# Spreading the dense steps of four tiles among the gathered blocks of the other sixteen in a two-layer graph network

## The chip, the cores and the metric

The kernel runs on one core of one Trainium2 chip. The metric is the device time of one execution in microseconds (us). Several executions are timed and their median is taken; one more execution is recorded by the hardware profiler.

## What is computed

The input is a node matrix x of 2500 rows and 1024 columns, 80,000 edges (`src`, `dst`, `edge_weight`, sorted by `dst`), and two 1024 x 1024 weights. The destinations are drawn as the square of a uniform number, so that low rows receive many edges and high rows few. Two layers follow each other:

```python
h = relu(layernorm(x))
x = x + segment_sum((h @ W0)[src] * edge_weight[:, None], dst)      # layer 0
h = relu(layernorm(x)) @ W1.T + b
deg = 1 + count of edges with row = src
x = x + segment_sum(norm[:, None] * h[col], row)                    # layer 1, with self loops
# row, col = src, dst and the self loops; norm = deg[row] ** -0.5 * deg[col] ** -0.5
```

Everything is float32.

## The kernel before, in words

The 2500 rows are 20 tiles of 128 rows (the last has 68). The work runs in four parts.

The first part, up to about 477 us, normalises each tile of x, multiplies it by W0 (`products`, L277) and stores the result to `support` in DRAM. At the same time the edges are laid out in blocks of 128 edges, each block belonging to one destination tile. `TILE_BLOCKS` gives the number of blocks of each tile: 146, 62, 48 and 41 for tiles 0 to 3, then 36 down to 10 for tiles 4 to 19.

The second part aggregates layer 0. It visits the tiles in `ORDER`. Each has an accumulator `sums` of 128 x 1024 in PSUM (two banks, pool name `mm`, two such buffers). There are two ways to fill it:

- The tiles 4 to 19 (378 blocks in all) are **gathered**. For each block GpSimd issues an indirect DMA that brings 128 rows of `support` into a `msg` buffer of 512 KB (L558). VectorE makes a one-hot matrix `oh_r` (L562); ScalarE multiplies the rows by the edge weights and rounds to `hi` (L564); VectorE makes the rest `lo` (L566); TensorE multiplies the one-hot matrix with both, in halves of 512 columns: four matmuls (L570).
- The tiles 0 to 3 are **dense**. For them a matrix of 128 destination rows by 2500 source rows has been counted and weighted beforehand (`dense`). For each of 20 source tiles SyncE loads 512 KB of `support` into a `msg` buffer of the same eight, and TensorE does two float32 matmuls (L583). A dense step has no work for VectorE, ScalarE or GpSimd.

When a tile's sums are complete, `finish` adds them to x (`xt`, L539), stores x1, takes the moments and normalises (`hn`, L140), transposes (L530, through the PSUM buffers `pT`), multiplies by W1 (sixteen float32 matmuls, L277, into a buffer `mm`), adds the bias (L549) and stores `hid`. `finish` is a generator: its pieces are issued among the steps of the next tile.

Throughout the first two parts VectorE also counts edges per pair of rows (`count_group`, L432, L434, L444, with matmuls L436 and, for dense tiles, L448). `count` decides by a small clock model (`takes`) when the next group of blocks is counted. `fences` with `BEHIND` keep a step's first matmul behind the counts that were issued five steps earlier.

The third part (L645 to L649) reads `hid` back, scales it by `dis` and splits it in `hi` and `lo`. The fourth (L675) multiplies the stored counts with them, tile by tile, and writes the output.

The order of the work in the second part is thus written out in Python by the loops over `ORDER`; the framework's scheduler then settles each engine's instruction order, the buffers and the waits. SyncE issues all plain DMAs of this part in one queue: `msg` loads of dense steps, `xt` loads, the stores of x1 and `hid`, and the stores of counts (`cnat`). GpSimd issues the gathers.

Of the kernel before, what the change touches and what calls it, by code (L numbers as in the profile page):

```python
# [9 lines left out]
F32 = mybir.dt.float32  # L10
# [9 lines left out]
P = 128  # L20
# [12 lines left out]
DENSE = 4  # L33

LEAD = 4.0

BEHIND = 5

ORDER = (3, 4, 5, 6, 2, 7, 8, 9, 1, 10, 11, 12, 13, 0, 14, 15, 16, 17, 18, 19)

# [2 lines left out]
def direct(  # L43
# [26 lines left out]
    nc = tc.nc  # L70
    N, D = x.shape
    E = src.shape[0]
    NT = -(-N // P)
# [59 lines left out]
    def normed(xt, pool):  # L133
        mv = moments(xt, pool)
        rstd = pool.tile([P, 2], F32, name="rstd")
        nc.scalar.activation(rstd[:, 0:1], mv[:, 1:2], AF.Sqrt, bias=eps)
        nc.vector.reciprocal(rstd[:, 0:1], rstd[:, 0:1])
        nc.vector.scalar_tensor_tensor(rstd[:, 1:2], mv[:, 0:1], -1.0, rstd[:, 0:1], op0=ALU.mult, op1=ALU.mult)
        hn = pool.tile([P, D], F32, name="hn")
        nc.scalar.activation(hn, xt, AF.Relu, scale=rstd[:, 0:1], bias=rstd[:, 1:2])  # L140
        return hn
# [132 lines left out]
    def product(vT, ws, mm):  # L274
        for h in range(2):
            for k in range(KC):
                on_pe(nc.tensor.matmul(mm[:, h, :], vT[:, k, :], ws[k][:, h * H:(h + 1) * H],  # L277
                                       start=(k == 0), stop=(k == KC - 1)))
                if k % 2:
                    yield  # L280
# [192 lines left out]
    def left(queue):  # L473
        return sum(b - a for _, _, a, b in queue)
# [56 lines left out]
            nc.scalar.copy(into[:, k0:k0 + 4, :], pT)  # L531
            yield 0.7, 0.0, 0.6

    PIECES = 11

    def finish(t, sums):

        xt = load_rows(t, work)
        nc.vector.tensor_add(xt, sums.rearrange("p h d -> p (h d)"), xt)  # L539
        nc.sync.dma_start(x1_d[t], xt)  # L540
        hn = normed(xt, work)
        yield 0.0, 3.4, 1.5
        vT = work.tile([P, KC, P], F32, name="vT")
        yield from transposed(hn, vT)
        mm = psum.tile([P, 2, H], F32, name="mm")
        for _ in product(vT, w1_sb, mm):
            yield 1.75, 0.0, 0.0
        hid = work.tile([P, D], F32, name="hn")
        nc.vector.tensor_add(hid, mm.rearrange("p h d -> p (h d)"), bias)  # L549
        nc.sync.dma_start(hid_d[t], hid)  # L550
        takes(v=1.25)

    def gathered(t, sums):
        n = TILE_BLOCKS[t]
# [32 lines left out]
                    on_pe(i)  # L587
            yield 1.75, 0.0, 0.0

    waiting = iter(())  # L590
    todo, steps = left(to_count[1]), [NT * 4 if t < DENSE else TILE_BLOCKS[t] for t in ORDER]
    done = 0
    w1_sb = []
    for t in ORDER:
        sums = psum.tile([P, 2, H], F32, name="mm")
        pieces = 0.0
        for took in (multiplied if t < DENSE else gathered)(t, sums):
            k = len(w1_sb)
            if k < KC:
                w1_sb.append(wpool.tile([P, D], F32, name=f"w{k}"))  # L600
                nc.sync.dma_start(w1_sb[k], w1t[k * P:(k + 1) * P, :])
            pieces += 1.15 * PIECES / (NT if t < DENSE else TILE_BLOCKS[t])
            done += 4 if t < DENSE else 1
            while pieces >= 1:
                takes(*next(waiting, (0.0, 0.0, 0.0)))
                pieces -= 1
            count(*took, least=todo * (1 - 1.05 * done / sum(steps)))
        for took in waiting:
            takes(*took)
        if t == ORDER[0]:  # L610
            nc.sync.dma_start(bias, b1.rearrange("(o d) -> o d", o=1).to_broadcast([P, D]))
        waiting = finish(t, sums)
    for queue in to_count:
        while queue:
            count_next(queue)
    store_counts(late=False)
    for _ in waiting:
        pass


    nc.vector.tensor_reduce(deg, total, axis=mybir.AxisListType.X, op=ALU.add)
# [399 lines left out]
```

## Time and profile before

| what | us |
|---|---|
| median of 3 executions | 1795.9 (1795.83 to 1800.01) |
| the profiled execution | 1796.9 |
| its span in the trace | 1795.0 |
| TensorE busy | 1685.8 |
| VectorE busy | 1209.5 |
| ScalarE busy | 900.2 |
| GpSimd busy | 494.5 |
| first dense matmul starts | 482.4 |
| last W1 product ends | 1407.2 |

The ends of the tiles in the second part can be read from the starts of the add to x (L539): 529.7 for the dense tile 3, then 591.0, 647.6 and 696.4 for tiles 4 to 6, 753.3 for the dense tile 2, and so on up to 1386.2 for tile 19.

The profile names a line of the code, an engine, an operation and the tiles it writes and reads. A float32 matmul shows as two records. The busy time of TensorE comes from modelled ends of matmuls that overlap, so the distance between the starts of neighbouring matmuls tells more about its speed than the length of one. "Granted clock" is the share of TensorE's full clock in a window. A line "A <- B: t, n, m" in a list of waits says that A stood idle for t us in all, n times, at most m us, until B had finished.

### The profile page before, as it was taken

Reading aid. Unit: us, or ns where it says so; the run is one execution under the profiler, and the core shown is the slowest. Engines: PE = TensorE matmul, PEld = TensorE weight load, DVE = VectorE, ACT = ScalarE, POOL = GpSimd, SP = SyncE. Lnnn points to the kernel's source line nnn. Section 1 sums busy time; section 2 is a strip of 40 time slices with the busy share of each in tenths; the row PEclk is TensorE's granted clock in tenths of the full one; section 3 lists DMA queues with packets and bytes.
Section 4 is the critical chain, followed back from the end, with each engine's and each line's share of the span. In section 5 each row is a group of like instructions: output and inputs, shape, how many; then the busy total and the mean of one; then the engine's idle time right before and its main releaser. Section 6 shows DMA issues by size and latency. Waiting matters only on the chain.

```text
span 1795.0 us, 21337 instructions
## 1 busy us (share of the span) xinstructions
PE 1685.8 (94%) x6506; PEld 1047.4 (58%) x6506; DVE 1209.5 (67%) x3031; ACT 900.2 (50%) x1476; POOL 494.5 (28%) x457
## 2 busy tenths in 40 slices
PE   6999999999899999999999999989998999999998
PEld 2465655544345555456645555455554668888886
DVE  5887988898698997999988997188886330000000
ACT  3499999961136773276515665166564431111110
POOL 3000000000036771377416773266661000000000
PEclk9999999999899999999999999999999999999999
DMA  7513121132788999799979999788884764242420
GB/s 255 191 40 97 48 77 60 39 83 71 244 285 319 366 340 324 229 338 328 348 242 323 321 315 333 246 307 312 310 300 167 216 191 104 77 114 76 115 62 32
DMA packets 217330, 369.97 MB, mean 206 GB/s; under 512 B 115662, under 2 KB 135128, under 8 KB 217206
## 3 DMA queue, kind: packets, MB, share of 16 engines
q0 software_dynamic: 54832, 199.25, 31.9%
q1 hardware_dynamic: 162374, 169.25, 30.3%
q8 instruction: 54, 0.88, 0.2%
q14 instruction: 70, 0.57, 0.1%
HBM read 300.79 MB, written 54.56 MB: 198 GB/s over the span
## 4 chain that ended last, share of the span: by engine, by line
PE 53%; DVE 7%; DMA 1%; issue 1%; ACT 1%; DVEq 0%; ACTq 0%
PE mm L675 18%; PE mm L570 14%; PE mm L277 13%; PE mm L583 5%; DVE lo L566 3%; DMA rows<-hid_d 1%; PE pT L530 1%; DVE stats L128 1%; DVE xt L539 1%; PE cb L436 1%; DVE lo L649 1%; DVE oh_r L562 0%; ACT hi L647 0%; DVE counts L444 0%; DVE hn L549 0%
## 5 line engine op out<-in xcount | busy, mean ns | idle before, releaser
L558 POOL DMA_INDIRECT msg<-support,src_p x378 | 479.1, 1268 | 493.6 <-PE cb L436 129.0
L564 ACT ACTIVATE hi<-msg,wgt_p 128x1024 fp32r<-128x1024 f32 x378 | 424.2, 1147 | 315.8 <-PE mm L570 194.3
L566 DVE SCALAR_TENSOR_TENSOR lo<-msg,wgt_p,hi 128x1024 fp32r<-128x1024 f32 x378 | 477.0, 1279 | 78.6 <-ACT hi L564 77.0
L570 PE MATMUL mm<-lo,oh_r 128*128 128x512 f32 x756 | 285.1, 459 | 37.8 <-DVE lo L566 37.5
L277 PE MATMUL mm<-w,hT 128*128 128x512 f32 x640 | 317.4, 608 | 2.4 <-ACT hT L169 2.4
L277 PE MATMUL mm<-w,vT 128*128 128x512 f32 x640 | 307.6, 594 | 0.0
L570 PE MATMUL mm<-hi,oh_r 128*128 128x512 f32 x756 | 291.4, 468 | 15.5 <-DVE oh_r L562 9.9
L441 ACT ACTIVATE wl<-oh_low,wpart 128x128 bf16<-128x128 bf16 x891 | 261.9, 410 | 0.0
L675 PE MATMUL mm<-hi,bT 128*128 128x512 f32 (+1 forms) x800 | 249.2, 394 | 3.6 <-ACT bT L657 2.0
L675 PE MATMUL mm<-lo,bT 128*128 128x512 f32 (+1 forms) x800 | 249.4, 394 | 3.0 <-DVE lo L649 2.6
L663 DVE SCALAR_TENSOR_TENSOR rows<-mm,dis,rows 128x1024 f32<-128x1024 f32 x20 | 25.7, 1283 | 309.0 <-PE mm L675 308.9
L570 PEld LDWEIGHTS mm<-lo,oh_r 128*128 128x128 f32 x756 | 139.9, 197 | 127.8 <-DVE lo L566 83.1
L570 PEld LDWEIGHTS mm<-hi,oh_r 128*128 128x128 f32 x756 | 147.2, 199 | 99.4 <-ACT hi L564 41.3
L434 DVE TENSOR_SCALAR oh_key<-iota,key 128x200 bf16<-128x200 f16 (+12 forms) x675 | 193.1, 289 | 3.1 <-PE cb L448 2.8
L444 DVE TENSOR_TENSOR counts<-cb,counts 128x200 f32 (+13 forms) x296 | 138.5, 469 | 59.1 <-PE cb L436 52.8
L657 ACT CAST bT<-cT 128x2560 fp32r<-128x2560 f16 x20 | 46.6, 2335 | 262.2 <-PE mm L675 258.8
L675 PEld LDWEIGHTS mm<-lo,bT 128*128 128x128 f32 (+1 forms) x800 | 150.6, 190 | 39.5 <-DVE lo L649 8.1
L675 PEld LDWEIGHTS mm<-hi,bT 128*128 128x128 f32 (+1 forms) x800 | 151.4, 190 | 37.2 <-ACT bT L657 2.4
L277 PEld LDWEIGHTS mm<-w,vT 128*128 128x128 f32 x640 | 121.0, 190 | 86.6 <-issue 71.8
L432 DVE TENSOR_SCALAR oh_low<-iota,low 128x128 bf16<-128x128 f16 x675 | 164.6, 247 | 6.9 <-PE cb L436 5.5
L583 PE MATMUL mm<-msg,dense 128*128 128x512 f32 (+1 forms) x320 | 150.1, 599 | 5.6 <-DMA msg<-support 5.2
L277 PEld LDWEIGHTS mm<-w,hT 128*128 128x128 f32 x640 | 109.2, 195 | 64.6 <-issue 58.0
(141 smaller groups left out, 1135.2 us busy)
## 6 DMA issues: line engine op xcount, KB each, us to landing
msg<-support SPq DMA_DIRECT2D x76, 512.0 KB, 5.2
xt<-in_x SPq DMA_DIRECT2D x38, 512.0 KB, 7.1
cnat<-counts SPq DMA_DIRECT2D x20, 640.0 KB, 5.6
x_d<-xt SPq DMA_DIRECT2D x20, 512.0 KB, 7.4
hid_d<-hn SPq DMA_DIRECT2D x20, 512.0 KB, 6.2
rows<-hid_d SPq DMA_DIRECT2D x20, 512.0 KB, 4.5
rows<-x_d SPq DMA_DIRECT2D x20, 512.0 KB, 4.3
hT<-in_xT SPq DMA_DIRECT2D x19, 512.0 KB, 4.4
```

The lines of the kernel that those rows point to most:

```text
L277: on_pe(nc.tensor.matmul(mm[:, h, :], vT[:, k, :], ws[k][:, h * H:(h + 1) * H], start=(k == 0), stop=(k == KC - 1)))
L432: nc.vector.tensor_scalar(oh_low, iota16[:, :P], low[:, k:k + 1], None, op0=ALU.is_equal)
L434: nc.vector.tensor_scalar(oh_key[:, :NT * w], iota16[:, :NT * w], key[:, k:k + 1], None, op0=ALU.is_equal)
L441: nc.scalar.activation(wl[:, i, :], oh_low, AF.Copy, scale=wpart[:, i, k:k + 1])
L444: nc.vector.tensor_tensor(to, cb[:, :NT * w].rearrange("p (t w) -> p t w", w=w), to, op=ALU.add)
L558: nc.gpsimd.indirect_dma_start(out=msg, out_offset=None, in_=support, in_offset=bass.IndirectOffsetOnAxis(ap=src_p[:, k:k + 1], axis=0))
L564: nc.scalar.activation(hi, msg, AF.Copy, scale=wgt_p[:, k:k + 1])
L566: nc.vector.scalar_tensor_tensor(lo, msg, wgt_p[:, k:k + 1], hi.bitcast(F32), op0=ALU.mult, op1=ALU.subtract)
L570: i = nc.tensor.matmul(sums[:, h, :], oh, v[:, h * H:(h + 1) * H], start=(j == 0 and v is hi), stop=(j == n - 1 and v is lo))
L583: i = nc.tensor.matmul(sums[:, h, :], dense[t][:rows(k), k, :], msg[:rows(k), h * H:(h + 1) * H], start=(k == 0), stop=(k == NT - 1))
L657: nc.scalar.copy(bT, cT)
L675: nc.tensor.matmul(mm[:, h, :], bT[:rows(k), k, :], v[:rows(k), h * H:(h + 1) * H], start=(k == ORDER[0] and v is his[k]), stop=(k == ORDE ...
```

## The change

The loop over `ORDER` is replaced by a plan. `thick` are the dense tiles and `thin` the gathered ones, each in the order of `ORDER`. The plan is a list of booleans, true for a dense step: eight dense steps first (`OPENING`), then after the blocks of each thin tile a number of dense steps in proportion to its blocks, all used up 48 blocks before the last one (`TAIL`). Of a tile's dense steps all but two are spread between its blocks, and two follow its last block. Two generators deliver the steps of the two kinds, so that one dense and one gathered `sums` are open at the same time.

`finish` now runs its first piece (the load of x, the add and the store of x1) as soon as the last step of a tile is issued; the rest goes into a list `waiting`, from which pieces are taken at a rate that allows for the dense tiles finished meanwhile. The product with W1 goes by halves of 512 columns, each in one of the two `pT` banks, each with its own add of the bias, instead of one `mm` buffer of two banks and one add of 1024 columns.

The loads of W1, issued with the first steps before, are issued with the eight steps after the eight dense ones; the load of `bias` follows them.

```diff
+OPENING = 8
+TAIL = 48
...
-    PIECES = 11
+    PIECES = 12
 
     def finish(t, sums):
 
         xt = load_rows(t, work)
         nc.vector.tensor_add(xt, sums.rearrange("p h d -> p (h d)"), xt)
         nc.sync.dma_start(x1_d[t], xt)
+        yield 0.0, 1.25, 0.0
         hn = normed(xt, work)
-        yield 0.0, 3.4, 1.5
+        yield 0.0, 2.2, 1.5
         vT = work.tile([P, KC, P], F32, name="vT")
         yield from transposed(hn, vT)
-        mm = psum.tile([P, 2, H], F32, name="mm")
-        for _ in product(vT, w1_sb, mm):
-            yield 1.75, 0.0, 0.0
         hid = work.tile([P, D], F32, name="hn")
-        nc.vector.tensor_add(hid, mm.rearrange("p h d -> p (h d)"), bias)
+        for h in range(2):
+            mm = psum.tile([P, 4, P], F32, name="pT").rearrange("p a b -> p (a b)")
+            for k in range(KC):
+                on_pe(nc.tensor.matmul(mm, vT[:, k, :], w1_sb[k][:, h * H:(h + 1) * H],
+                                       start=(k == 0), stop=(k == KC - 1)))
+                if k % 2 and k < KC - 1:
+                    yield 1.75, 0.0, 0.0
+            nc.vector.tensor_add(hid[:, h * H:(h + 1) * H], mm, bias[:, h * H:(h + 1) * H])
+            if h == 0:
+                yield 1.75, 0.65, 0.0
         nc.sync.dma_start(hid_d[t], hid)
-        takes(v=1.25)
+        yield 1.75, 0.65, 0.0
...
-    waiting = iter(())
-    todo, steps = left(to_count[1]), [NT * 4 if t < DENSE else TILE_BLOCKS[t] for t in ORDER]
+    thick, thin = [t for t in ORDER if t < DENSE], [t for t in ORDER if t >= DENSE]
+    blocks = sum(TILE_BLOCKS[t] for t in thin)
+    plan = [True] * OPENING
+    rate = [0.0] * OPENING
     done = 0
+    for t in thin:
+        n = TILE_BLOCKS[t]
+        done += n
+        m = min(DENSE * NT, OPENING + -(-(DENSE * NT - OPENING) * done // (blocks - TAIL))) - sum(plan)
+        inner = max(m - 2, 0)
+        for j in range(n):
+            plan.append(False)
+            plan += [True] * ((j + 1) * inner // n - j * inner // n)
+        plan += [True] * (m - inner)
+        rate += [1.1 * PIECES * (1 + m / NT) / (n + m)] * (n + m)
+    assert sum(plan) == DENSE * NT
+
+    waiting = []
+    todo = left(to_count[1])
     w1_sb = []
-    for t in ORDER:
-        sums = psum.tile([P, 2, H], F32, name="mm")
-        pieces = 0.0
-        for took in (multiplied if t < DENSE else gathered)(t, sums):
-            k = len(w1_sb)
-            if k < KC:
+
+    def steps_of(tiles):
+        for t in tiles:
+            sums = psum.tile([P, 2, H], F32, name="mm")
+            n = NT if t < DENSE else TILE_BLOCKS[t]
+            for j, took in enumerate((multiplied if t < DENSE else gathered)(t, sums)):
+                if j == n - 1:
+                    rest = finish(t, sums)
+                    takes(*next(rest))
+                    waiting.append(rest)
+                yield took
+
+    kinds = {True: steps_of(thick), False: steps_of(thin)}
+    pieces = 0.0
+    for i, is_dense in enumerate(plan):
+        took = next(kinds[is_dense])
+        if i == OPENING:
+            for k in range(KC):
                 w1_sb.append(wpool.tile([P, D], F32, name=f"w{k}"))
-                nc.sync.dma_start(w1_sb[k], w1t[k * P:(k + 1) * P, :])
-            pieces += 1.15 * PIECES / (NT if t < DENSE else TILE_BLOCKS[t])
-            done += 4 if t < DENSE else 1
-            while pieces >= 1:
-                takes(*next(waiting, (0.0, 0.0, 0.0)))
-                pieces -= 1
-            count(*took, least=todo * (1 - 1.05 * done / sum(steps)))
-        for took in waiting:
-            takes(*took)
-        if t == ORDER[0]:
+        if i >= OPENING and (i - OPENING) < KC:
+            nc.sync.dma_start(w1_sb[i - OPENING], w1t[(i - OPENING) * P:(i - OPENING + 1) * P, :])
+        if i == OPENING + KC:
             nc.sync.dma_start(bias, b1.rearrange("(o d) -> o d", o=1).to_broadcast([P, D]))
-        waiting = finish(t, sums)
+        pieces = min(pieces + rate[i], 2.0) if waiting else 0.0
+        while pieces >= 1 and waiting:
+            piece = next(waiting[0], None)
+            if piece is None:
+                waiting.pop(0)
+                continue
+            takes(*piece)
+            pieces -= 1
+        count(*took, least=todo * (1 - 1.05 * (i + 1) / len(plan)))
...
-    for _ in waiting:
-        pass
+    for rest in waiting:
+        for _ in rest:
+            pass
```

## The prediction

> **What bounds the kernel now.** I first read the busy shares on the page, then a table of windows cut at the ends of tiles, then TensorE's waits, then the order of time around one tile's end.
>
> ```profile
> PE 1685.8 (94%) x6506; PEld 1047.4 (58%) x6506; DVE 1209.5 (67%) x3031; ACT 900.2 (50%) x1476; POOL 494.5 (28%) x457
> ```
>
> TensorE looks full, but the share hides that it alternates between two kinds of hunger. In the table by tiles (busy time of PE, PEld, DVE, ACT, POOL, then granted clock, DMA share, GB/s):
>
> ```profile
> 591.00:647.00 56.00, 51.56 (x182) 33.25 (x183) 55.33 (x88) 40.95 (x39) 43.18 (x36) 0.97 0.95 353
> ...
> 696.00:753.00 57.00, 56.80 (x170) 26.10 (x169) 45.40 (x145) 9.43 (x8) 8.43 (x9) 1.00 0.77 249
> ...
> 1114.00:1164.00 50.00, 50.00 (x125) 22.74 (x124) 7.87 (x14) 5.00 (x6) 8.66 (x10) 1.00 0.77 265
> ...
> 1204.00:1242.00 38.00, 34.42 (x120) 21.08 (x118) 32.85 (x47) 23.98 (x24) 25.82 (x21) 1.00 0.89 311
> ```
>
> Row 591 is gathered tile 5: VectorE is busy 55.3 of 56 us, TensorE waits, DMA moves 353 GB/s. Rows 696 and 1114 are dense tiles 2 and 0: TensorE is full, VectorE idles 11.6 and 42.1 us, DMA is at 0.77. The change mixes these two. What TensorE waits for from 482 to 1409 us:
>
> ```profile
> PE mm L570 <- DVE lo L566: 37.5, 56, 1.9
> PE mm L570 <- DVE oh_r L562: 9.9, 18, 0.7
> PE mm L583 <- DMA msg<-support: 5.2, 1, 5.2
> PE pT L530 <- ACT hn L140: 5.1, 1, 5.1
> PE mm L570 <- ACT hi L564: 4.3, 1, 4.3
> ```
>
> With three small rows this is 65.6 us. Where it falls is seen in TensorE's order of time at the end of tile 15:
>
> ```profile
> 1243.81 0.70 PE L570 MATMUL mm<-hi,oh_r 128*128 128x512 f32 x2 [0.69 <-DVE oh_r L562]
> 1246.10 0.73 PE L570 MATMUL mm<-lo,oh_r 128*128 128x512 f32 x2 [1.59 <-DVE lo L566]
> ...
> 1247.56 1.22 PE L570 MATMUL mm<-lo,oh_r 128*128 128x512 f32 x2 [0.26 <-DVE lo L566]
> 1248.58 1.05 PE L570 MATMUL mm<-hi,oh_r 128*128 128x512 f32 x2
> 1249.43 1.05 PE L570 MATMUL mm<-lo,oh_r 128*128 128x512 f32 x2
> ```
>
> VectorE adds the finished tile to x and takes moments (L539, L128), the next blocks stand behind it, TensorE starves 2.5 us, and then pairs of matmuls start 0.85 us apart instead of 0.46: half speed for 3 us.
>
> **What the Trainium skill says.** "TensorE: Matmul & The Clock Gate", Part 1: the array's clock is halved when an activity window of about 3.4 us was too idle, and restored after a busy one. The trace agrees: the 0.85 us pairs above last 3 us, clock is 1.00 in dense windows and 0.93 to 0.97 in most gathered ones. "DMA: Bandwidth & Descriptors", Anatomy of one DMA: a DMA's semaphore wait is done by the issuing sequencer before dispatch, so what is behind it on that queue waits too. The trace agrees: SyncE's own waits hold
>
> ```profile
> SPq L550 <- DVE oh_r L562: 340.8, 14, 41.8
> ```
>
> that is, hid's store stands at the queue's head for up to 41.8 us. Same page, Bandwidth: 358 GB/s per core from HBM; here 353 over 56 us, so gathered windows are near it.
>
> **Durations.** From starts in the order of time: a gathered matmul 0.23 us, four a block (chain of waits: x8 in 1.85); a dense or W1 matmul 0.86 (x4 records, two calls, in 1.72); a transpose 0.25; a count 0.16. VectorE: lo 1.20, one-hot 0.20, so 1.40 a block; add to x 1.14; two stats 1.19; add of bias 1.14 (profiled 1.215).
>
> **The change part by part.**
> *Total work.* The built orders have the same matmuls: 1512 gathered, 160 dense, 320 W1, 160 transposes. TensorE saves only waits and half clock. VectorE gets 20 more instructions: two half adds by 0.65 (nearest: the 512-wide stats, 0.68) for one of 1.215, 20 x 0.09 to 0.14 = 2 to 3 us; part of the sum below.
>
> *The pool.* Of 65.6 us of waits, 5.2 are the opening DMA, 8.3 lie in 1282 to 1386 (tiles 17 to 19, the 48-block tail that keeps no dense steps), 6.6 at the end. 45.5 remain in the middle. Clock: length times (1 - clock) over the windows from 530 to 1282 gives 20.0 us. The pool is 65.5 us.
>
> *Dense steps spread.* 80 steps, 8 first, then 8, 8, 6, 6, 6, 6, 5, 5, 5, 4, 5, 4, 4 per thin tile. Check on tile 15 (20 blocks): now 38.7 us, plus 4 of 20 steps of a dense stage of some 50 us = 48.7. Mixed: TensorE 20 x 0.92 + 4 x 1.72 + 1.2 finishes x 15.8 (16 x 0.86 + 8 x 0.25) = 44.3; VectorE 20 x 1.40 + 1.2 x 4.2 (add, stats, small ones, bias) = 33. TensorE leads; a saving of 4.4 at best. For tile 5 (33 blocks, 8 steps): now 56.5 + 0.4 x 55 = 78.5; TensorE 30.4 + 13.8 + 1.4 x 15.8 = 66.3; VectorE 46.2 + 5.9 + counts of some 0.5 us a block = 69. But the mix inside a tile is uneven: in the built order the late tiles still have some 13 blocks with few W1 products, then 7 with all sixteen. So I walked both orders from the first dense step to the last W1 product in stretches of equal numbers of blocks, added each engine's work with the durations above, and took the larger. Stretches of four: before 925 (the trace, 482.4 to 1407.2: 925), after 905. Of eight: 899 and 875. So -20 to -24 (lengths 5 to 7: -23 to -27). I take -23, half of the 45.5. In it is the end: 8 W1 products of tile 18 (6.9 us) now stand before the last transposes and cover the 5.1 us wait for hn.
> *Clock.* If half of the starving goes, half of the 20.0: -10. Bounds 0 (gaps merely become rarer, windows still under the threshold) and -20.
> *Second product by halves.* Sixteen matmuls as before, now in pT's two banks; the two mm buffers are left to one dense and one thin sum. New wait: the next thin tile's first matmul needs the add to x of the last one (before, it started at 1242.39, while the add ran from 1242.26). Cover in the built order: dense steps, two to four calls (1.7 to 3.4 us) in the most places, against 1.2 for the add and up to 1.2 more if a lo is in the way. The three changes of dense tile have gathered blocks as cover. Behind a late add TensorE's whole queue waits. 0 to +1 us at 16 places: I take +3.
> *DMA queues.* 72 dense loads move among hid's, x1's and xt's issues on SyncE. In the built order each stands behind a store whose producer is 5 to 47 us of TensorE work ahead of its use; six have under 8 us, against 5.1 from issue to landing and 0.32 to issue. 0 to +3 us each: I take +2. POOL: gathers share the eight msg buffers with the dense loads; 20 blocks and 4 loads in 45 us is the buffer rate that row 1204 already has (20 in 38.7). 0. Bytes are unchanged: 279 MB from 480 to 1400, 303 GB/s; 28 us less needs 313.
> *W1's loads.* In the built order six still precede the first dense load and two follow the eighth, nearly as before (two after the seventh and eighth): no change. 0; their cover is tile 4's blocks, as the first W1 product comes after it.
> Sum: -23 - 10 + 3 + 2 = -28. The profiled execution took 1796.9 us (span 1795.0 and 1.9 around it): 1769; the median stands 1.0 lower: **1768 us**.
>
> **Rivals.**
> 1. *The whole pool goes:* no waits nor half clock in the middle, and the end's 5.1: up to -65; VectorE would have to be at 90%. More likely -45: 1751. For: row 1114's 42 idle VectorE us. Against: gathered stretches without W1 products remain.
> 2. *Slower: the dense loads come late through SyncE's single queue.* A load behind a store of hid that waits for its product stops TensorE by the lateness, and half clock adds 1.7 us. With 13 mixed tiles and a gain of 33, it decides from 2.5 us per tile, half clock included; at 3 + 1.7, +61 - 33 = +28: 1824. For: the 340.8 us above. Against: the slack in the built order.
> 3. *DMA limits:* the mixed stage is all at the gathered load. If it can't sustain over the 305 GB/s of rows 1164 to 1321, 279 MB take 915 us against 920: -5: 1791.
> 4. *It doesn't do what it says:* true of W1's loads already, price 0.
>
> **How the numbers follow.** Forecast (-12 to -40) 0.62, rival 1 0.13, rival 3 (within some 8 us) 0.14, rival 2 0.11. The range 1748 to 1793 leaves out rival 2, and the far end of rival 1. Some 0.3% (5.4 us) is what a measurement can tell from no change. Faster: 0.62 + 0.13 + 0.05 of rival 3 = 0.80; same 0.09; slower 0.11.
>
> **What would show it.** Right: L570's wait for lo down to some 20 us, clock of the middle 0.98, DVE at 85% or more in every window from 500 to 1280 with DMA at 0.9 throughout, the last gathered product near 1358 instead of 1386, and the wait for hn at the end gone. Wrong: waits of L594 (dense) for DMA in many places (rival 2), ACT's hi waiting for msg (rival 3), or the same 2.5 us starving at each tile's end.

## The result and the profile after

The changed kernel takes 1793.4 us (median of 20 executions, 1782.08 to 1800.28); the kernel before took 1798.0 in 20 executions beside it. The ratio is 0.9975, 95% interval 0.9958 to 0.9992: faster by 4.6 us, inside the 0.3% that the prediction called no change. The forecast was 1768 with a range from 1748 to 1793. The profiled execution took 1799.5 us, its span 1797.5.

Lines have moved: the gathered matmuls are L581 (L570 before), the dense ones L594 (L583), hi and lo L575 and L577, the add to x L543, the dense loads L592, W1's product L554, the clearing of counts L422 (L418), their store L497 (L493).

Busy time of the engines, from the page of the changed kernel:

```profile
PE 1674.1 (93%) x6506; PEld 1036.6 (58%) x6506; DVE 1207.7 (67%) x3051; ACT 903.0 (50%) x1476; POOL 479.4 (27%) x457
```

TensorE has the same instructions as before and is busy 11.7 us less, in a span that is 2.5 us longer. So it waits more, not less. Windows of the second part (length, busy time of PE, PEld, DVE, ACT and POOL, granted clock, DMA share, GB/s):

```profile
600.00:700.00 100.00, 82.25 (x270) 48.16 (x269) 75.06 (x143) 51.36 (x48) 47.00 (x37) 0.91 0.79 279
...
800.00:900.00 100.00, 89.48 (x293) 51.70 (x294) 84.30 (x175) 49.41 (x48) 48.66 (x40) 0.93 0.84 286
900.00:1000.00 100.00, 100.00 (x344) 59.26 (x344) 95.75 (x190) 58.19 (x56) 50.90 (x43) 1.00 0.92 323
1000.00:1100.00 100.00, 89.45 (x288) 52.28 (x287) 81.82 (x163) 46.04 (x45) 49.02 (x38) 0.93 0.81 277
```

From 900 to 1000 us the stage is what the forecast wanted: TensorE full, VectorE at 96%, DMA at 0.92. In the other three rows TensorE, VectorE and the DMA engines sag together, so no one of them is full: something makes all of them wait. What TensorE waits for, from 477 to 1420 us:

```profile
PE mm L594 <- DMA msg<-support: 38.9, 12, 6.3
PE mm L581 <- DVE lo L577: 16.0, 35, 2.1
PE mm L581 <- ACT hi L575: 14.6, 5, 10.6
PE mm L581 <- DVE xt L543: 4.3, 4, 1.6
```

The waits for VectorE have gone as forecast: lo from 37.5 to 16.0, oh_r's 9.9 and hn's 5.1 out of the list. Two others stand in their place. The dense matmuls wait for their loads, 38.9 us (5.2 before; in the middle, from 510 to 1287 us, 33.5 against none), and one wait for hi is 10.6 us long.

**The late dense load.** SyncE's order of time around one of them:

```profile
612.42 0.33 SPq L561 DMA_DIRECT2D hid_d<-hn  x1
615.67 0.32 SPq L592 DMA_DIRECT2D msg<-support  x1
```

and TensorE's at its use:

```profile
618.51 0.70 PE L581 MATMUL mm<-hi,oh_r 128*128 128x512 f32 x2
623.21 2.04 PE L594 MATMUL mm<-msg,dense 128*128 128x512 f32 x2 [4.00 <-DMA msg<-support]
624.26 1.84 PE L581 MATMUL mm<-lo,oh_r 128*128 128x512 f32 x2
```

The load is issued 3.3 us after a store of hid on the same queue. TensorE arrives at 619.2, only 3.5 us after the issue, stands still for 4.0 us, and starts 7.5 us after the issue. The next pairs start 1.05 and 1.64 us apart, against 0.45 and 0.88 for the same two kinds of pair at 615.5: about half speed.

The other late loads are like it. If each load of SyncE's order is set beside the first matmul that reads it, 19 of the 72 loads after the opening are issued less than 8 us before TensorE arrives (the shortest lead is 3.1 us); in the kernel before, none has under 11.0. The eleven of the middle that come late had 3.1 to 7.3 us, and their matmuls started 5.4 to 13.6 us after the issue (median 7.7; the landings of the other loads can't be read). So these loads were both issued late and slow to land. For the slowest, issued at 840.82, the DMA records show a reason: a store of counts, issued at 837.21 on the same queue, was still moving until 845.3, and no 4 KB packet of that queue started between the load's issue and 845.5.

SyncE's own waits say what holds such loads back (477 to 1400 us):

```profile
SPq L592 <- DMA msg<-support,src_p: 114.8, 20, 13.7
SPq L544 <- DVE xt L543: 109.4, 13, 17.2
SPq L592 <- DVE lo L577: 107.6, 21, 11.8
```

The loads' own waits (L592) are for a msg buffer that the gathers share: they ended, as the profile infers it, with the landing of a gather or with a lo that read its rows. In between stand stores that wait for their producers (L544).

**The long wait for hi.** ScalarE's order of time, then TensorE's, then the one line of SyncE's that matters:

```profile
677.51 1.15 ACT L575 ACTIVATE hi<-msg,wgt_p 128x1024 fp32r<-128x1024 f32 x1 [0.34 <-DMA msg<-support,src_p]
688.22 2.32 ACT L422 CAST counts<-zero 128x2560 f16<-128x2560 f32 x1 [9.56 <-DMA cnat<-counts]
690.45 2.19 ACT L575 ACTIVATE hi<-msg,wgt_p 128x1024 fp32r<-128x1024 f32 x2
```

```profile
691.64 1.22 PE L581 MATMUL mm<-hi,oh_r 128*128 128x512 f32 x2 [10.57 <-ACT hi L575]
```

```profile
667.72 0.43 SPq L497 DMA_DIRECT2D cnat<-counts  x1
```

ScalarE is to clear a buffer for the next tile's counts, and the counts that lie in it have not yet left: their store was issued at 667.72 and, by the DMA records, its last of 2560 packets of 256 bytes ended at 687.8. All hi products stand behind the clearing. In the kernel before the same wait is longer, and TensorE goes on beside it:

```profile
498.49 2.32 ACT L418 CAST counts<-zero 128x2560 f16<-128x2560 f32 x1 [23.49 <-DMA cnat<-counts]
513.88 2.32 ACT L418 CAST counts<-zero 128x2560 f16<-128x2560 f32 x1 [13.06 <-DMA cnat<-counts]
```

```profile
498.41 1.88 PE L583 MATMUL mm<-msg,dense 128*128 128x512 f32 x4
500.12 0.77 PE L436 MATMUL cb<-oh_key,oh_low 128*128 128x360 bf16 x4
500.74 1.88 PE L583 MATMUL mm<-msg,dense 128*128 128x512 f32 x4
```

There it falls into a pure dense stretch, in which TensorE needs nothing from ScalarE. Once only, in gathered tile 4, does a clearing of the kernel before hold TensorE up; this is the 4.3 us of waiting for hi that the prediction lists:

```profile
547.59 2.32 ACT L418 CAST counts<-zero 128x2560 f16<-128x2560 f32 x1 [4.63 <-DMA cnat<-counts]
```

```profile
551.01 1.22 PE L570 MATMUL mm<-hi,oh_r 128*128 128x512 f32 x2 [4.30 <-ACT hi L564]
```

### The profile page after: what moved, and what is told of

It is laid out like the page before. It is cut to its first block, busy times and chain, and to the rows that moved or that the text cites. A ratio compares the mean times of both kernels' runs of the same rounds, so it can differ in the third digit from the quotient of the medians.

```text
span 1797.5 us, 21334 instructions
## 1 busy us (share of the span) xinstructions
PE 1674.1 (93%) x6506; PEld 1036.6 (58%) x6506; DVE 1207.7 (67%) x3051; ACT 903.0 (50%) x1476; POOL 479.4 (27%) x457
## 5 line engine op out<-in xcount | busy, mean ns | idle before, releaser
L575 ACT ACTIVATE hi<-msg,wgt_p 128x1024 fp32r<-128x1024 f32 x378 | 426.1, 1147 | 375.9 <-PE mm L581 281.1
L569 POOL DMA_INDIRECT msg<-support,src_p x378 | 464.1, 1228 | 515.2 <-DVE lo L577 178.0
L577 DVE SCALAR_TENSOR_TENSOR lo<-msg,wgt_p,hi 128x1024 fp32r<-128x1024 f32 x378 | 478.7, 1281 | 94.9 <-ACT hi L575 54.2
L581 PE MATMUL mm<-hi,oh_r 128*128 128x512 f32 x756 | 291.0, 466 | 19.9 <-ACT hi L575 14.6
L554 PE MATMUL pT<-w,vT 128*128 128x512 f32 x640 | 303.1, 595 | 0.0
L581 PE MATMUL mm<-lo,oh_r 128*128 128x512 f32 x756 | 280.4, 451 | 16.9 <-DVE lo L577 16.0
L594 PE MATMUL mm<-msg,dense 128*128 128x512 f32 (+1 forms) x320 | 166.6, 636 | 38.9 <-DMA msg<-support 38.9
L581 PEld LDWEIGHTS mm<-hi,oh_r 128*128 128x128 f32 x756 | 141.7, 192 | 103.2 <-issue 46.4
L581 PEld LDWEIGHTS mm<-lo,oh_r 128*128 128x128 f32 x756 | 138.3, 192 | 102.8 <-DVE lo L577 49.5
L554 PEld LDWEIGHTS pT<-w,vT 128*128 128x128 f32 x640 | 120.8, 190 | 94.5 <-issue 80.4
L436 DVE TENSOR_SCALAR oh_low<-iota,low 128x128 bf16<-128x128 f16 x675 | 168.3, 253 | 1.3 <-ACT wl L445 1.1
```

The source lines that it names most:

```text
L436: nc.vector.tensor_scalar(oh_low, iota16[:, :P], low[:, k:k + 1], None, op0=ALU.is_equal)
L554: on_pe(nc.tensor.matmul(mm, vT[:, k, :], w1_sb[k][:, h * H:(h + 1) * H], start=(k == 0), stop=(k == KC - 1)))
L569: nc.gpsimd.indirect_dma_start(out=msg, out_offset=None, in_=support, in_offset=bass.IndirectOffsetOnAxis(ap=src_p[:, k:k + 1], axis=0))
L575: nc.scalar.activation(hi, msg, AF.Copy, scale=wgt_p[:, k:k + 1])
L577: nc.vector.scalar_tensor_tensor(lo, msg, wgt_p[:, k:k + 1], hi.bitcast(F32), op0=ALU.mult, op1=ALU.subtract)
L581: i = nc.tensor.matmul(sums[:, h, :], oh, v[:, h * H:(h + 1) * H], start=(j == 0 and v is hi), stop=(j == n - 1 and v is lo))
```

## The experiments

All ratios are to the kernel before, run on the same chip. Two things set how finely builds can be told apart: the intervals are 0.2 to 0.7% wide, and E16 below, whose program hardly differs from the changed kernel, came out 0.5% below it. So a difference between two builds of under some 9 us isn't counted as shown unless a line of the trace carries it.

My theory after reading the two traces was that the spread is worth what was forecast and that late dense loads take it back. Rivals: the transfer rate, SyncE's queue alone, the shared buffers alone, or a spread that brings nothing.

### E1: the dense loads left out

```diff
-            msg = gpool.tile([P, D], F32, name="msg", bufs=8)
-            nc.sync.dma_start(msg[:rows(k), :], support[k * P:k * P + rows(k), :])
+            if t == ORDER[0] and k < OPENING:
+                msg = gpool.tile([P, D], F32, name="msg", bufs=8)
+                nc.sync.dma_start(msg[:rows(k), :], support[k * P:k * P + rows(k), :])
+            else:
+                msg = w1_sb[0]
```

> The changed kernel, but the 72 dense steps after the first eight don't load rows of support: they multiply by a resident tile of W1 in place of them, so layer 0's dense sums are not the reference's. Every matmul, gather and store stays. If late dense loads are what took the gain (theories queue, buffers and bandwidth alike), TensorE's 33.5 us of waits for them in the middle go, the 10.6 us wait for a late gather too, and some 10 to 20 us of half clock: 40 to 60 us faster than before, 1740 to 1757. If the dense waits only stand where TensorE would else wait for VectorE, lo's wait grows back to 30 us and the time stays at 1780 or above.

Measured: 1729.0 us, ratio 0.9611 (0.9587 to 0.9635). TensorE's waits from 510 to 1287 us:

```profile
PE mm L581 <- ACT hi L575: 9.0, 1, 9.0
PE mm L581 <- DVE lo L577: 7.2, 14, 1.6
```

Without load costs the new order is fast. One wait for hi of 9.0 us is left, which dense loads can't explain. It ends just after a clearing that waited for a store of counts:

```profile
664.94 2.32 ACT L422 CAST counts<-zero 128x2560 f16<-128x2560 f32 x1 [9.29 <-DMA cnat<-counts]
```

### E12: the same loads left out of the order before

The kernel before with the second product by halves (E4), and E1's edit.

> Control for the run that left out the loads of the changed kernel: the kernel before with the second product by halves alone (dense tiles in one piece), with the same 72 dense loads left out and a resident tile of W1 read in their place, so part of the sums is left out. Halves with loads: 1790 us. Theory A (spreading the dense steps is worth its forecast some 30 to 45 us where the loads cost nothing): 1765 to 1785 us here, so 35 to 55 above the spread without loads (1729). Rival D (the 70 us came from leaving traffic out, whatever the order): 1725 to 1745 us here, within 15 us of the spread.

Measured: 1777.3 us, ratio 0.9896 (0.9874 to 0.9919). TensorE's waits, 510 to 1287 us:

```profile
PE mm L574 <- DVE lo L570: 27.8, 46, 1.6
PE mm L574 <- DVE oh_r L566: 5.2, 8, 0.7
```

E1 against E12 is the worth of the spread alone: **48 us** by the medians (51 by the ratios), as theory A said. Leaving the loads out of the old order brings only some 12 us over E4.

### E11: the loads' traffic without their buffers and waits

```diff
+                msg = w1_sb[0]
+                spare = dram.tile([P, D], F32, name=f"spare{t}_{k}")
+                nc.sync.dma_start(spare[:rows(k), :], support[k * P:k * P + rows(k), :])
```

> The changed kernel with 72 of its 80 dense loads (all beyond the first eight) replaced by copies of the same rows into scratch memory in DRAM that nobody reads; the dense matmuls then read a resident tile of W1 in place of the rows, so part of the second-stage sums is left out. The traffic of the loads stays, at the same places of SyncE's program; the buffers and the waits are gone. Left out entirely the loads gave 1729 us (ratio 0.961). Theory A (buffers and lateness): 1728 to 1745 us, ratio 0.96 to 0.97, hi's wait on TensorE under 12 us. Rival B (transfer rate: the traffic itself slows gathers): 1770 to 1790 us, ratio over 0.983, ScalarE's hi waiting for DMA well over the 25 us of the changed kernel.

Measured: 1738.5 us, ratio 0.9678 (0.9657 to 0.9699). The traffic costs some 9 to 12 us against E1; with the buffers and waits too, the changed kernel is 64 us above E1. So the transfer rate falls as the main cause. One thing E11 can't tell: how long a load takes to land beside the gathers, as nobody waits for these copies.

### E2: the dense loads on GpSimd's queue

```diff
-            nc.sync.dma_start(msg[:rows(k), :], support[k * P:k * P + rows(k), :])
+            nc.gpsimd.dma_start(msg[:rows(k), :], support[k * P:k * P + rows(k), :])
```

> The changed kernel with the dense loads issued by GpSimd, in one queue with the gathers, not by SyncE behind the stores of x1 and hid. Theory queue (a load stands behind a store that waits for its product): waits of dense matmuls for DMA fall from 33.5 to under 10 us, the time to 1755 to 1770. Theory buffers (the load waits for one of the eight shared msg buffers): about as late as now, 1785 to 1798. Theory bandwidth (the load takes 7 to 9 us to land beside gathers): unchanged, 1790 to 1798. GpSimd has the room: it is busy half of the middle and an issue costs it about 1 us, 80 in all.

Measured: 1791.2 us, ratio 0.9953 (0.9936 to 0.9970).

```profile
PE mm L594 <- DMA msg<-support: 30.6, 11, 5.9
```

The dense loads are about as late as in the changed kernel, now behind gathers that wait for buffers. (The wait for hi is down to 1.9 us, but one of 7.0 for a count has come.) So SyncE's queue isn't the cause by itself. A queue in which nothing else waits was not tried.

### E3: two buffers of the dense loads' own, six for the gathers

```diff
     def gathered(t, sums):
...
-            msg = gpool.tile([P, D], F32, name="msg", bufs=8)
+            msg = gpool.tile([P, D], F32, name="msg", bufs=6)
...
     def multiplied(t, sums):
...
-            msg = gpool.tile([P, D], F32, name="msg", bufs=8)
+            msg = gpool.tile([P, D], F32, name="dmsg", bufs=2)
```

> The changed kernel with the eight msg buffers parted: six for gathers, two for dense loads; SyncE still issues. Theory buffers: a load waits no longer for a gathered block's buffer, dense waits fall to 10 us or less, 1760 to 1775, if six buffers are enough for the gathers; with too few, ScalarE's hi waits for msg more. Theory queue: the loads still stand behind the stores, 1785 to 1798. Theory bandwidth: unchanged, 1790 to 1798.

Measured: 1826.4 us, ratio 1.0155 (1.0127 to 1.0182). Waits, 510 to 1287 us:

```profile
PE mm L594 <- DMA dmsg<-support: 36.2, 15, 8.7
PE mm L581 <- ACT hi L575: 23.5, 10, 7.9
```

A miss. Gathers lost two buffers and now hi is late as well, and the dense loads didn't come sooner.

### E4: the second product by halves, alone

The kernel before with only the change in `finish` that makes W1's product in two pT banks.

> The kernel before with only the second product by halves in the pT banks; the order of tiles and steps as before. By the prediction halves cost 0 in themselves: 1793 to 1800, ratio 0.998 to 1.001. A rival: the pT banks are held by a half until VectorE has added it, so that the next transposes wait, 1800 to 1810; another: the mm buffer set free gives part of the gain by itself, 1785 to 1792.

Measured: 1790.4 us, ratio 0.9964 (0.9949 to 0.9979). This part alone comes out where the whole change does, 6 to 8 us under the kernel before, which is less than the 9 us that two builds can differ by. Why it is a gain and not the small loss that I had priced, the runs don't settle: the waits for lo (31.0 us from 510 to 1287) are hardly shorter than before (32.9), those for oh_r are 6.4 against 9.2, for hi 1.3 against 4.3.

### E5 to E8: six and ten msg buffers in both orders

`bufs=8` becomes 6 or 10 in both places. For ten, the pool of the counting's one-hot matrices shrinks from eight to four buffers to make room, which delays the first dense matmul by 52 to 55 us in both orders, so only the two orders of one size can be compared.

> The changed kernel with six msg buffers, not eight, shared by gathers and dense loads. Theory buffers (with the steps mixed, each transfer needs its buffer for the 7 to 9 us of landing and the steps before its turn, so eight are the limit of the mixed stage): the dense and gather waits grow much, +25 to +60 us on the changed kernel, 1818 to 1855. Theory bandwidth (the bytes per us are the limit): fewer buffers change little, +0 to +10.

> Second product by halves alone, tiles in the old order, with six msg buffers. Theory buffers: where gathers and dense steps don't mix, TensorE and VectorE are late for other reasons, so six cost less than in the changed kernel: +3 to +20 us on the halves alone (1793 to 1810). If it grows as much as in the changed kernel, the sharing isn't what makes the mixed stage need buffers.

> The changed kernel with ten msg buffers; the room comes from four one-hot buffers of the counting in place of eight. Theory buffers: the dense waits of 33 us and hi's of 15 us at least halve, 1755 to 1775, if four one-hot buffers don't slow the counts. Theory bandwidth: unchanged, 1788 to 1798.

> Second product by halves alone, old order, ten msg buffers and four one-hot buffers: shows what four one-hot buffers cost and what ten msg buffers bring without the mixing. Theory buffers: within 5 us of the halves alone, 1785 to 1796. If it gains as much as the changed kernel does from ten, the buffers are no matter of mixing.

| msg buffers | spread | halves alone | difference |
|---|---|---|---|
| 6 | 1.0282 (1.0248 to 1.0316) | 1.0172 (1.0138 to 1.0205) | +0.0110 |
| 8 | 0.9975 (0.9958 to 0.9992) | 0.9964 (0.9949 to 0.9979) | +0.0011 |
| 10 | 1.0203 (1.0169 to 1.0237) | 1.0281 (1.0247 to 1.0315) | -0.0078 |

E5 came out as expected; E6 lost 37 us on E4 where 3 to 20 were expected, and E7 and E8 came out far above what was expected, for the most part by the later start. Each two buffers help the spread by 0.9 to 1.0% (16 to 18 us) more than they help the old order. Each such figure takes four builds, so this points to the buffers as a part of it without showing it; and with ten the dense matmuls still wait 28.5 us.

### E9, E10: the dense matrices' freed slots for the loads

A dense tile's matrix of 10 KB per partition isn't needed once the tile is done. E9 puts the later tiles' loads there, as two views of 4 KB for each finished tile, and leaves all eight msg buffers to the gathers. E10 also writes each of these loads as far ahead as there are views (the `while` below is in E10 only).

```diff
+            if k == NT - 1 and t != 0:
+                freed = dpool.tile([P, NT, P], F32, name="dense").rearrange("p t w -> p (t w)")
+                views[:0] = [freed[:, :D], freed[:, D:2 * D]]
+            while views and len(early) < len(views) and k + NT * (3 - t) + len(early) + 1 < DENSE * NT:
...
+                nc.sync.dma_start(view[:rows(n), :], support[n * P:n * P + rows(n), :])
+                early.append(view)
```

> The changed kernel, but once dense tile 3 is done its matrix's 10 KB slot of the dense pool receives the dense loads of tile 2 (two views of 4 KB, used in turn), and likewise two more views for tile 1 and two more for tile 0. The gathers then keep all eight msg buffers for themselves from the end of tile 3 on; nothing else moves, the dense loads stand at the same places of SyncE's program. Theory A (the dense loads come late because they take buffers from the gathers and wait for them): dense matmuls' wait for DMA between 510 and 1290 us falls from 33.5 to under 15 us, the gathered products' wait for hi from 14.6 to under 10, half clock from 55 to under 40 us, time 1760 to 1780 us (ratio 0.98 to 0.99). Rival B (transfer rate: the DMA engines beside the gathers carry no more): dense waits stay at 25 to 40 us, ratio 0.993 to 1.00. Rival C (lateness comes from the place of the loads in SyncE's program behind stores, buffers don't matter): dense waits fall by a few us only here, and fall to under 10 in the run where the loads are written ahead.

> As the freed slots, and each of these loads is written as far ahead as there are views: right after the dense step that last read the view, so two dense steps ahead in tile 2, four in tile 1, six in tile 0, before the stores and rows of the tiles between. Theory A (buffers alone): no better than the freed slots within 3 us. Rival C (program order on SyncE): dense waits between 510 and 1290 us under 10 us, and 5 to 20 us better than the freed slots; together about 1750 to 1770 us. Rival B (transfer rate): dense waits still 20 us or more or the same time lost as gathered waits for msg instead (ScalarE's hi waiting for DMA above the 25 us of the changed kernel, TensorE's wait for hi above 15), ratio 0.99 to 1.00.

Measured: E9 1785.7 us, ratio 0.9935 (0.9915 to 0.9955); E10 1775.1 us, ratio 0.9880 (0.9861 to 0.9898). Waits from 510 to 1287 us, E9 and then E10:

```profile
PE mm L600 <- DMA dense<-support: 24.4, 5, 9.7
PE mm L581 <- ACT hi L575: 11.8, 4, 9.3
...
PE mm L600 <- DMA msg<-support: 4.9, 3, 3.4
```

```profile
PE mm L581 <- ACT hi L575: 23.5, 4, 10.7
PE mm L600 <- DMA dense<-support: 10.9, 4, 4.2
...
PE mm L600 <- DMA msg<-support: 4.9, 3, 3.5
```

Buffers of their own, without a loss for the gathers, aren't enough (E9: 29.3 us of waits for loads, and 7 us below the changed kernel, which by itself shows nothing). With an earlier place in SyncE's program as well, the waits for loads are 15.8 us: 4.9 in tile 3, which still uses msg, 10.9 in tile 2, whose loads are two steps ahead, and none in tiles 1 and 0, with four and six. E10 is 17 us below the changed kernel. The earlier place with the shared buffers was not run, so the two aren't parted on that side. And hi's wait has grown to 23.5 us: ScalarE's clearing of counts waits longer for stores in this stretch of E10 than the 15.1 us of the changed kernel.

```profile
ACT counts L422 <- DMA cnat<-counts: 36.2, 4, 12.0
```

### E13, E14: a fourth buffer for the counts

```diff
+            turn.append(t)
-            counts[t] = cpool.tile([P, NT, P], F16, name="counts")
+            counts[t] = cviews[0] if cviews and len(turn) % 4 == 0 else cpool.tile(
+                [P, NT, P], F16, name="counts")
```

E13 does this in the changed kernel, with a view of tile 3's freed matrix; E14 in E10, where that slot then holds one view for loads and one for counts.

> The changed kernel with a fourth buffer for the counts (a view of dense tile 3's matrix, free once that tile is done) beside the three of the pool; every fourth tile of counts uses it. The dense loads stay as they are. Theory E (ScalarE's clearing of the next counts tile waits for an earlier tile's slow store of counts; before the change that wait fell in pure dense stretches where ScalarE had nothing else to do, and now it holds up the products hi of the gathered blocks): between 510 and 1290 us ScalarE's wait of the clearing falls from 15.1 us to under 5, TensorE's wait for hi from 14.6 to under 5 us, time 6 to 14 us shorter than the changed kernel (1780 to 1788, ratio 0.990 to 0.994). Rival (hi is late because its msg is late, the store is only what the record shows last): wait for hi stays over 10 us, ratio 0.996 to 0.999.

> The freed slots with loads written ahead (1775 us), tile 3's slot now shared by one view for dense loads of tile 2 and a fourth counts buffer; tiles 1 and 0 have their two further views each as before. Theory E and the load theory together: TensorE's waits between 510 and 1290 us fall from 58 to about 35 us, hi under 8, 1755 to 1768 us (ratio 0.977 to 0.984). If hi's lateness has another cause: 1772 to 1780 us (ratio 0.986 to 0.991).

Measured: E13 1793.8 us, ratio 0.9979 (0.9964 to 0.9994), no gain. The ratio and hi's 10.6 us lie where the rival put them, but ScalarE's order of time shows that it wasn't a test: the extra buffer went to another tile's counts, and the clearing in question still waits.

```profile
679.98 2.32 ACT L425 CAST counts<-zero 128x2560 f16<-128x2560 f32 x1 [9.17 <-DMA cnat<-counts]
```

E14 1797.1 us, ratio 0.9992 (0.9978 to 1.0007), 20 us worse than E10. With one view instead of two, tile 2's loads can be written only one step ahead, and the wait for loads into freed slots is back, all of it in tile 2:

```profile
PE mm L603 <- DMA dense<-support: 30.4, 11, 5.5
```

against E10's 10.9. Hi's wait is down to 4.1 us, but two edits are in this run. It shows how much the second view in tile 2 is worth, and leaves the counts open.

### E15, E17, E18: the counts stored at once

The store of a tile's counts is written one step after its last sum, not six.

```diff
-            to_store.append([6, t])
+            to_store.append([1, t])
```

E17 does only this in the changed kernel, E15 in E10, E18 in the halves alone.

> The freed slots with loads written ahead, and the store of a tile of counts is written one step after its last sum and not six. Theory E: the store starts some 5 us sooner, of ScalarE's waits of 10 to 12 us for it half goes, 1765 to 1773 us (ratio 0.983 to 0.987). Rival (SyncE then stands still at the store until VectorE has made the sum, and the dense loads behind it come late): dense waits rise above the 16 us of that kernel, ratio 0.988 to 0.995.

> The changed kernel with the one edit of the stores of counts: written one step after the last sum and not six; dense loads as they are in the changed kernel. With loads ahead this edit brought 26 us (1775 to 1749). Theory E (ScalarE's clearing waits for the store, in the changed kernel too): TensorE's wait for hi between 510 and 1290 us falls from 14.6 to under 6 us, and the half clock goes with it: 1765 to 1785 us (ratio 0.981 to 0.992). Rival (in the changed kernel the loads on SyncE stand behind that store, which now waits for VectorE, and lose what the clearing gains): ratio 0.993 to 1.001, wait for dense loads above the 33.5 us of the changed kernel.

> The halves alone (dense tiles in one piece, 1790 us) with the same one edit of the stores of counts. Theory E (in the order before, ScalarE's waits for those stores lie in dense stretches and cost nothing): within 4 us of the halves alone, ratio 0.994 to 0.999. Rival (the late stores cost the same in either order, so they are no part of what took the gain back): 1765 to 1775 us, ratio 0.983 to 0.988.

| order | store after six steps | at once | difference |
|---|---|---|---|
| changed kernel (E17) | 0.9975 | 0.9873 (0.9839 to 0.9907) | -18 us |
| loads ahead (E10, E15) | 0.9880 | 0.9727 (0.9703 to 0.9752) | -28 us |
| order before, halves (E4, E18) | 0.9964 | 0.9976 (0.9964 to 0.9988) | +2 us |

That is theory E in all three rows: a gain of this size from the store's place came only in the new order. In the old order the edit removed one long clearing wait, in dense tile 1, without a gain (E4, then E18):

```profile
917.22 2.33 ACT L418 CAST counts<-zero 128x2560 f16<-128x2560 f32 x1 [20.88 <-DMA cnat<-counts]
```

```profile
908.23 2.32 ACT L418 CAST counts<-zero 128x2560 f16<-128x2560 f32 x1 [1.61 <-DMA cnat<-counts]
```

The long ones of the opening stayed (24.1 us in E4, 18.7 and 21.0 in E18), so for these E18 is no test; that TensorE works on beside them is read from the trace. In E17 the trace has

```profile
PE mm L594 <- DMA msg<-support: 23.1, 10, 5.8
...
PE mm L581 <- ACT hi L575: 2.5, 2, 1.3
```

from 510 to 1287 us: hi 2.5 instead of 14.6, and the wait for loads 10 us shorter too. How the store's place helps the loads, no run shows, so the 18 us aren't all the clearing's. The clearings of counts between 580 and 700 us waited 2.9 and 9.6 us in the changed kernel, here none and 6.2. E15, **1749.2 us**, beats both kernels and its own forecast: 2.7% faster than the one before, and its windows come near to what the forecast asked for:

```profile
600.00:700.00 100.00, 90.88 (x308) 54.81 (x307) 84.70 (x160) 53.83 (x51) 54.49 (x44) 0.97 0.88 318
800.00:900.00 100.00, 95.49 (x323) 56.55 (x322) 93.49 (x189) 57.25 (x53) 55.86 (x43) 0.98 0.92 327
...
1000.00:1100.00 100.00, 97.89 (x335) 57.24 (x334) 95.85 (x188) 53.27 (x55) 55.76 (x42) 1.00 0.96 343
```

Its waits from 510 to 1287 us are

```profile
PE mm L581 <- DVE lo L577: 9.8, 23, 1.6
PE mm L600 <- DMA dense<-support: 8.0, 4, 4.4
```

with 7.4 us for hn, 3.4 for msg and 3.3 for hi.

### E16: W1's loads put back

```diff
-        if i == OPENING:
+        if i == 0:
             for k in range(KC):
                 w1_sb.append(wpool.tile([P, D], F32, name=f"w{k}"))
-        if i >= OPENING and (i - OPENING) < KC:
+        if i < KC:
```

> The changed kernel with W1's loads put back among the first eight dense steps, as in the kernel before. The prediction's price for that move was 0 (rival 4: up to 28 us hang on it). With price 0: ratio 0.995 to 1.000, within 4 us of the changed kernel. With a real price: 1800 us or more, TensorE's wait for the second to the eighth dense load growing.

Measured: 1787.5 us, ratio 0.9927 (0.9903 to 0.9952). In SyncE's order only one of the eight loads stands elsewhere (one place earlier), and one load of x has changed places with a store of hid. That such a program comes out 8.6 us below the changed kernel, with its waits for dense loads at 27.6 instead of 33.5 us, says how much the mixed stage depends on chance in the order; it isn't the worth of W1's loads.

## Why the prediction was wrong

The time moved the forecast way by 4.6 us and not by 28. The last gathered product starts at 1389.4 us, 3 us later than before and not 28 earlier. Step by step:

*Stretch sums (-23) and clock (-10).* Right in mechanism, too small rather than too large together: E12 to E1 is -48 where the loads cost nothing. Some 22 us of it are waits (from 482 to 1380 in E12 and to 1336 in E1, TensorE is busy 849.8 of 898 and 828.0 of 854 us), about the forecast's 23. Another 22 are busy time for the same matmuls. Of these the granted clock explains some 9, near the forecast's 10: it is 0.981 over the 1773.1 us of E12 and 0.986 over the 1728.3 us of E1, so by my estimate half clock costs 34 and 24 us. The remaining 13 or so stay open. In the changed kernel itself the clock step failed, because the lost time reappears in gaps of 4 to 10 us, and these bring half clock with them: 0.91 and 0.93 in three of the windows above, where I had forecast 0.98. Over the whole middle the clock is no better than before (the kernel before, then the changed one):

```profile
510.00:1287.00 777.00, 728.57 (x2395) 428.19 (x2394) 662.13 (x1168) 424.20 (x407) 431.67 (x341) 0.97 0.89 310
```

```profile
510.00:1287.00 777.00, 710.71 (x2341) 415.51 (x2340) 649.31 (x1180) 414.07 (x393) 401.17 (x325) 0.96 0.87 304
```

"TensorE: Matmul & The Clock Gate", Part 1, in the Trainium skill puts the halving on a too idle window of some 3.4 us; the trace agrees in that the gaps of 4.0 and 10.6 us were followed by pairs at half speed.

*DMA queues (+2). This step failed.* I had read from the built order how far ahead of its use a load's predecessor on SyncE was made, and found "six have under 8 us". I compared that with 5.1 us from issue to landing, about the median of the kernel before, most of whose dense loads land while few gathers run (8.4 us of GpSimd's work in the 57 us of tile 2). The built program didn't keep the leads that I had read from it: 19 loads were issued under 8 us ahead, not six. And 5.1 us was too short beside gathers. With the leads that the eleven late loads had, 5.1 us would have made them 6 us late in all (estimate: the sum of what each lead lacks to 5.1); they were 33.5 us late, because they took 5.4 to 13.6 us. And I priced the shared msg buffers at 0, from the rate at which they turn over; but a rate isn't a lead. A dense load that has to wait for a buffer, in a queue whose next entry waits too, gets whatever lead is left. The runs: 33.5 us of waits in the middle; GpSimd's queue doesn't help (E2), buffers taken from the gathers make it worse (E3), buffers from elsewhere help little (E9), and buffers together with an earlier place win back 17 us (E10). How much of the slow landing comes from the gathers' share of the DMA engines isn't measured.

*ScalarE and the counts: not in the prediction.* I counted SyncE's loads and stores and named "the stores of counts" only in the description. The 4.3 us of waiting for hi stood in my own list, and I didn't ask what made hi late. The prediction asked, for the removed stall, what is late next, and answered with VectorE's add to x. The right question was what the pure dense stretches were hiding: there ScalarE's waits of 13 to 23 us for the stores of counts had cost nothing. Spread out, the dense steps cover 2 us at a time. Writing the stores earlier won 18 us in the changed kernel (E17), 28 in E10 (E15), and nothing in the old order (E18).

*Second product by halves (+3).* The wait that I priced is there: 2.7 us for the add to x in the middle, 4.3 in all. But the part as a whole came out at -6 (E4), which is under the 9 us that two builds can differ by.

*W1's loads (0).* In the built order it is hardly a move, as I had said; E16 has no cost of it to show.

*The end.* Right: the wait of 5.1 us for hn after the last block is gone (0.3 us, for the last bias add, is left there), and the last gathered product is followed at once by sixteen W1 records.

*The rivals.* Rival 2 named a late dense load behind SyncE's stores, and that is what happened in kind. Its 3 us per wait came out too (33.5 us in eleven waits), but it set them and their half clock against a gain of 33, and the gain without load costs was 48. So the loads, together with the counts, cancelled the gain instead of reversing it. Its cause was half of the truth: off SyncE's queue the loads were as late (E2), and both buffers and place mattered. Rival 3, the DMA rate, gave the nearest number (1791) by luck: E11 prices the traffic at 9 to 12 us, and E15 carried more than its 305 GB/s.

The sum in the runs' own numbers: the halves alone 1790; the spread's 48 off makes 1742; measured 1793, so 51 us are lost. Loads ahead and counts stored at once win back 45 of them (E15: 0.9727 against 0.9975, times 1799). The remaining 6 to 7 are within what two builds differ by. The balance is rough, as E1, from which the 48 come, still has its wait of 9.0 us for hi.

## What to carry to other kernels

A stretch in which one engine works alone is idle time for the others, but it also absorbs their waits. Before such a stretch is dissolved, list every wait of every engine and queue that falls into it (here ScalarE's for a slow store, and the loads' for buffers) and price it as if it lay in the open. A load that is spread among other work needs its lead written into the program, with a buffer that it doesn't have to wait for: in tile 2 one step ahead left 30 us of waits and two steps 11, and in tiles 1 and 0 four and six steps left none.

## What the runs showed of the hardware

The store of counts, 640 KB in 2560 packets of 256 bytes, ended 4 to 6 us after its issue in the quiet first part (up to 440 us) and up to 20.1 us after it beside gathers. "DMA: Bandwidth & Descriptors", Why small descriptors are slow, reckons 27% overhead for packets of 256 bytes; the trace shows up to a factor of four between stores of the same packets, so that most of it is probably the sharing of the DMA engines with the gathers, which no run here measures by itself.

Also, the mixed stage carried 325 GB/s over 777 us (E15, 510 to 1287), where the kernel before had 310, and copies that nobody waited for, issued on the same queue, cost some 9 to 12 us. The prediction took 353 GB/s over 56 us for near the limit of a core; E10 moved 385 over as long a stretch, all transfers of the core together.

```profile
510.00:1287.00 777.00, 740.17 (x2491) 441.17 (x2491) 689.05 (x1244) 442.11 (x423) 444.37 (x350) 0.98 0.91 325
```

```profile
524.00:580.00 56.00, 46.35 (x153) 26.99 (x152) 49.16 (x80) 34.78 (x32) 36.19 (x30) 0.97 0.99 385
```
